# Graph attention on one core: edge values as one product with block-diagonal weights, and sums of two groups in tile pairs

## The chip, the cores and the metric

The kernel runs on one core of a Trainium2 chip. The metric is the device time of one execution in microseconds. Engines are named as the profile names them: PE is TensorE's matrix multiplication and PEld its weight load, DVE is VectorE, ACT is ScalarE, POOL is GpSimd, SP is the engine that issues most DMAs here. SBUF is the working memory of 128 partitions; PSUM is the small memory that PE writes, 128 partitions by 8 banks of 512 f32 values.

## What is computed

There are 6250 nodes with 64 features each and 206250 edges, sorted by destination. The reference, cut to what matters:

```
Qh = (x @ Wq.T + bq).reshape(n, 4, 16)      # Kh, Vh alike
Ee = (edge_attr @ We.T + be).reshape(-1, 4, 16)
score = (Kh[src] * Qh[dst] * (1.0 / np.sqrt(16)) * Ee).sum(-1)
score = jnp.exp(jnp.clip(score, -5.0, 5.0))
msg = Vh[src] * score[..., None]
wV = jax.ops.segment_sum(msg, dst, num_segments=n)
x = layernorm(x + wV.reshape(n, 64))
```

Two pieces matter for the change: the edge values Ee, a product of every edge's 64 attributes with a 64x64 matrix, and the sum of the messages over the edges of one destination.

## The kernel before, in words

Edges are cut into 1612 tiles of 128 edges. Eight tiles make a group, so there are 202 groups, the last with four tiles. Two groups make a step (97 such steps, written s < ONES; after them come 8 steps of one group, which the change leaves alone except for where their operands lie). One long unrolled loop runs over the groups, and the order of all instructions is the order in which the code is written: every engine works through its own queue in that order, and a framework adds the waits on semaphores. It also orders two accesses of different engines to one bank of a PSUM tile, even where they touch different columns.

For group g the work is spread over several turns of the loop (the lines are those of the profile):

- `edges(g)` (line 762) computes the edge values on PE, three turns ahead. The attributes lie transposed: tile 2i in partitions 0 to 63 and tile 2i+1 in partitions 64 to 127 of one 128x128 f32 block `ET`. The result goes to the PSUM region `ee`, of half a bank in each of two banks of the tile `room`. It takes four products: each has a 64x64 block of weights, 64 partitions of attributes and 256 columns (two tiles), and writes 64 partitions; the four use the four quarters of PE's array.
- `biased(g)` (771) adds the bias on ACT and copies to `EB`.
- `queries(g)` (778) computes the query of each edge on PE from a one-hot matrix `TO` (two products into `qq`), `terms(g)` (786) multiplies both on DVE, and `turn(g)` (792) transposes the product back, four 128x128 f32 transposes into `qe`.
- `products`, `weigh`, `message`, `keep` and `take` (820 to 862) form score and message on DVE and ACT. The message is written as three bf16 parts into `MSG`, so 192 columns for a tile.
- `onehot_edges(s)` (798) builds on DVE the one-hot matrices `OH` of a step, 64 destinations wide, by comparing `key` with a row of numbers. `keys` (278) prepares `key` 208 tiles at a time.
- `sums(s)` (874) adds the messages on PE: 16 products, for each of the 8 tile places j one of group 0 and one of group 1, each with 128x64 weights from `OH` and 192 columns of `MSG`. Group 0 writes partitions 0 to 63 and group 1 partitions 64 to 127 of the region `pa`, 192 columns in bank 0 of `room`. The loop gives them out in two halves of eight products.
- `add(s)` (903) reduces `pa` over the three parts on DVE (line 908) into 128x64 and adds it, masked, to two slots of a ring. `fold_blocks` and `add_blocks` (944, 957) carry the ring over to the result through `folded`, in bank 1 of `room`.

All PE products of the loop go through one helper, line 760, so the profile's rows for it are told apart by tile name and shape. The largest of them are the `pick` products: they fetch keys and values of some edges by one-hot matrices, 128x512 bf16, and in the loop they stand between the other products, two units of three products at a time (`picks`, 706). In the order of the queue a turn does: picks, then `turn(g+1)`, picks, `queries(g+2)`, `edges(g+3)`, picks, half of the sums, picks, the other half, picks. About every third turn, eight f32 products of 128 columns (`picked_kv`, 721, rows `pick<-w,x`) come at the turn's start. POOL gathers the other keys and values from memory; SP loads attributes, keys and single rows.

Of the kernel before, what the change touches and what calls it, by code (L numbers as in the profile page):

```python
# [12 lines left out]
AF = mybir.ActivationFunctionType  # L13
OP = mybir.AluOpType
AX = mybir.AxisListType

P = 128
N = 6250
C = 64
# [4 lines left out]
G = 8  # L24
# [3 lines left out]
NS = len(STEPS)  # L28
# [6 lines left out]
NR = P * NB  # L35
RING = 8
STEP = 31
SLACK = 14
SHIFT = STEP
TAIL = STEPS[ONES][0]  # L40
# [17 lines left out]
def tiles_of(g):  # L58
    return min(G, T - g * G)
# [86 lines left out]
def tile_gnn(ctx: ExitStack, tc: tile.TileContext, x, x_blocks, by_rows, xT, wT, bias, beT, weT, eT, src, src_rows,  # L146
             src_single, dst, dst_rows, out):
    nc = tc.nc
# [15 lines left out]
    dst_i = consts.tile([P, T], I32, name="dst_i")  # L164
# [15 lines left out]
    ident = consts.tile([P, P], F32, name="ident")  # L180
# [14 lines left out]
    key_i = consts.tile([P, KEYS], I32, name="key_i")  # L195
# [6 lines left out]
    we_sb = consts.tile([P, 2 * C], F32, name="we_sb")  # L202
# [5 lines left out]
    be_col = consts.tile([P, 1], F32, name="be_col")  # L208
# [13 lines left out]
    ET, QW, at = {}, {}, {}  # L222
    SRC, FROM, ODD, OVER, KB, TO = ({} for _ in range(6))
# [54 lines left out]
    def keys(t0):  # L278

        n = min(KEYS, T - t0)  # L280
        for lo, hi, rows in (t0, min(t0 + n, TAIL * G), C), (max(t0, TAIL * G), t0 + n, P):
            if lo < hi:
                nc.vector.tensor_scalar(key_i[:, lo - t0:hi - t0], dst_i[:, lo:hi], rows - 1, None,
                                        op0=OP.bitwise_and)
        nc.vector.tensor_copy(key[:, t0:t0 + n], key_i[:, :n, None].to_broadcast([P, n, 2]))

    def gather_kv(g, j):
# [29 lines left out]
    with tc.tile_pool(name="nodes", bufs=1) as nodes, \  # L317
# [27 lines left out]
        for i in range(NB // CB):  # L345
            s = slice(i * CB * P, (i + 1) * CB * P)
# [148 lines left out]
        for i in range(NB // CB):  # L495
            bs = slice(i * CB, (i + 1) * CB)
            kv_sb = chunks.tile([P, CB, 2 * C], F32, name="kv_sb")
            for b in range(0, CB, 2):
                two = slice(i * CB + b, i * CB + b + 2)
                ps = npsum.tile([P, 2, 3 * C], F32, name="ps")  # L500
                for u in range(2):
                    c0 = (i * CB + b + u) * P
                    mark.append(nc.tensor.matmul(ps[:, u, :], xT_sb[:, c0:c0 + P], w_sb, start=True,  # L503
                                                 stop=True))
# [137 lines left out]
    with tc.If(rv == 0) as branch:  # L642

        with tc.tile_pool(name="work", bufs=2) as work, \
# [3 lines left out]
            OH, OF, EB, TERM, MSG, SCORE, WEIGHT, HOT = ({} for _ in range(8))  # L648
# [4 lines left out]
            nc.tensor.transpose(still[:, C:C + NB].bitcast(BF16), half_b[:2 * NB].to_broadcast([2 * NB, P]),  # L653
                                ident_b[:2 * NB, :2 * NB])
            room = fixed.tile([P, 2, 4 * P], F32, name="room")
            ee = room[:, :, :2 * P].rearrange("p r (i e) -> p r i e", e=P)
            pa = room[:, 0, 2 * P:2 * P + 3 * C]
            folded = room[:, 1, 2 * P:2 * P + 2 * C].rearrange("p (b c) -> p b c", c=C)
            sum_ = still[:, 2 * P:2 * P + C]
            weights = [still[:, P + k * G * H:P + (k + 1) * G * H]  # L660
                       .rearrange("p (g h) -> p g h", g=G) for k in range(3)]
            px = [fixed.tile([P, 4 * P], F32, name=f"pick{k}") for k in range(2)]
            xs = [accp.tile([P, 4 * P], F32, name=f"x{k}") for k in range(2)]
            qq = fixed.tile([P, G // 2, P], F32, name="qq")
            qe = [fixed.tile([P, G, C], F32, name=f"qe{k}") for k in range(2)]
# [93 lines left out]
            def product(*aps, **kw):  # L759
                mark.append(nc.tensor.matmul(*aps, **kw))  # L760

            def edges(g):

                n = tiles_of(g) // 4
                for u in range(2):
                    for r in range(2):
                        rows = slice(r * C, (r + 1) * C)
                        product(ee[u * C:(u + 1) * C, r, :n, :], we_sb[rows, rows],
                                ET[g][rows, u * n:(u + 1) * n, :], start=True, stop=True)

            def biased(g):

                n = tiles_of(g) // 2
                EB[g] = work.tile([P, G // 2, P], F32, name="eb")
                nc.scalar.activation(EB[g][:, :n].rearrange("p (i r) e -> p r i e", r=2),  # L775
                                     ee[:, :, :n // 2], AF.Identity, bias=be_col)

            def queries(g):

                n = tiles_of(g)  # L780
                for u in range(2):
                    product(qq[u * C:(u + 1) * C, :n // 2, :], QW[g],
                                     TO[g][:, u * n // 2:(u + 1) * n // 2, :],
                                     start=True, stop=True)

            def terms(g):
# [5 lines left out]
            def turn(g):  # L792

                half = tiles_of(g) // 2
                for k in range(half):
                    nc.tensor.transpose(qe[g % 2][:, k:k + half + 1:half, :], TERM[g][:, k, :], ident)  # L796

            def onehot_edges(s):

# [69 lines left out]

            def pa_of(s):  # L870

                return {NS - 3: px[0][:, :3 * C], NS - 2: px[1][:, :C], NS - 1: qq.rearrange("p i e -> p (i e)")[:, :C]}.get(s, pa)

            def sums(s, some=slice(0, G)):
                n = tiles_in(s)
                if s < ONES:
                    for j in range(G)[some]:
                        for u in range(2):
                            t = u * G + j
                            product(pa[u * C:(u + 1) * C], OH[s][:, t, :],  # L880
                                    MSG[s][:, t].rearrange("p i c -> p (i c)"),
                                    start=j == 0, stop=j == G - 1, skip_group_check=True)
                    return
                for j in range(n):
                    product(pa_of(s), (OF if s >= WHOLE else OH)[s][:, j, :],
                            MSG[s][:, j].rearrange("p i c -> p (i c)") if s < WHOLE else MSG[s][:, j, :],
                            start=j == 0, stop=j == n - 1,
                                     skip_group_check=True)
# [14 lines left out]
            def add(s):  # L903
                b = first_row(s) // P
                what = pa_of(s)
                if s < ONES:
                    b = first_row(s) // C
                    nc.vector.tensor_reduce(sum_, what.rearrange("p (i c) -> p c i", i=3), axis=AX.X,  # L908
                                            op=OP.add)
                    for k, mask in ((b, above), (b + 1, below)):  # L910
                        slot = ring[:, k % RING, :]
                        if k in touched:
                            nc.vector.scalar_tensor_tensor(slot, sum_, mask_of(mask, s), slot,
                                                           op0=OP.mult, op1=OP.add)
                        else:
                            nc.vector.tensor_scalar(slot, sum_, mask_of(mask, s), None, op0=OP.mult)
                            touched.add(k)
                    return
                if s < WHOLE:
                    nc.vector.tensor_reduce(sum_, what.rearrange("p (i c) -> p c i", i=3), axis=AX.X,  # L920
                                            op=OP.add)
                    what = sum_
                for k, mask in ((b, above), (b + 1, below)):
                    if 0 <= k < BIG + 1:
                        slot = slot_of(k)
                        nc.vector.scalar_tensor_tensor(slot, what, mask_of(mask, s), slot,
                                                       op0=OP.mult, op1=OP.add)
# [92 lines left out]
            for g in range(NG + 1):  # L1020
# [65 lines left out]
                if g - 1 in ends and now:  # L1086
                    s = ends[g - 1]
# [235 lines left out]
```

## Time and profile before

| what | value |
|---|---|
| median of 3 runs | 2093.89 us |
| lowest and highest | 2090.95 and 2097.44 us |
| the profiled execution, its own time | 2090.01 us |
| its span, first to last instruction | 2088.2 us |
| mean granted TensorE clock | 0.947 |
| matmul records, weight load records | 10216, 10409 |

The profile is of one execution. Its lines of groups read: line, engine, operation, what it writes and reads, for a product rows*columns of the array and partitions x columns of the moving operand, how many; then busy microseconds in all and mean nanoseconds of one; then the engine's idle time just before such instructions and what ended it. A product's duration holds its way through the array, so back to back products overlap: what one costs PE is the distance from its start to the start of the next, which the timeline gives. An f32 product of this kernel leaves two records, two weight loads and two matmuls. "issue" is idle time whose end the profile explains by no semaphore.

### The profile page before, as it was taken

The numbers are of one execution on the slowest core, as the hardware profiler recorded it, in microseconds if no ns is written. First come the engines' busy times: TensorE is split into PE (matmuls) and PEld (weight loads), VectorE is DVE, ScalarE is ACT, GpSimd is POOL, SyncE is SP. The second block draws the span as 40 slices with busy tenths as digits, with TensorE's granted clock in tenths as the row PEclk, the third lists the DMA queues.
The fourth block names the chain that finished last, engine by engine and source line by source line (L and its number), as shares of the span: only waits on it lengthen the run. The fifth ranks groups of instructions, "written<-read, shape, count | busy, mean of one in ns | idle before, by whom it ended". The sixth has DMA issues, their size and how long they took to land.

```text
span 2088.2 us, 34475 instructions
## 1 busy us (share of the span) xinstructions
PE 1759.6 (84%) x10216; PEld 831.4 (40%) x10409; DVE 1538.9 (74%) x2598; ACT 1106.8 (53%) x1882; POOL 1254.1 (60%) x1333
## 2 busy tenths in 40 slices
PE   6588888888888889888898989888988988889994
PEld 6334343343334334333343334434433433334443
DVE  5477777777778678687777767767877787777886
ACT  3455555555555455455555545545655555555564
POOL 6566666666666666656666666656666666666542
PEclk9789999999999999999999999999999999999996
DMA  6524333332333333333233332333323333233320
GB/s 174 190 81 126 87 102 93 94 101 86 96 88 98 102 87 100 95 95 101 86 102 95 88 101 86 100 90 91 101 85 111 95 93 100 80 101 101 104 76 26
DMA packets 118968, 204.21 MB, mean 98 GB/s; under 512 B 57073, under 2 KB 60011, under 8 KB 118657
## 3 DMA queue, kind: packets, MB, share of 16 engines
q1 hardware_dynamic: 75998, 115.38, 17.8%
q0 software_dynamic: 42336, 85.48, 14.7%
q8 instruction: 83, 1.36, 0.3%
q10 hardware_dynamic: 436, 1.04, 0.2%
q14 instruction: 115, 0.94, 0.1%
HBM read 194.19 MB, written 7.59 MB: 97 GB/s over the span
## 4 chain that ended last, share of the span: by engine, by line
PE 70%; issue 13%; DVE 12%; ACT 2%; POOL 1%; another core or an unknown queue 1%; DMA 1%; DVEq 0%; ACTq 0%; POOLq 0%
PE pick L760 50%; PE room L760 11%; PE qe L796 4%; PE qq L760 3%; DVE hot L696 3%; DVE prod L822 1%; DVE msg L862 1%; DVE score L824 1%; POOL kv L289 1%; PE ps L503 1%; DVE term L790 1%; DVE qe L843 1%; DVE qe L862 1%; DVE of L810 1%
## 5 line engine op out<-in xcount | busy, mean ns | idle before, releaser
L289 POOL DMA_INDIRECT kv<-kv_tab,src_i x1283 | 1214.9, 947 | 783.8 <-issue 285.9
L760 PE MATMUL pick<-hot,parts 128*128 128x512 bf16 x4839 | 1241.5, 392 | 93.5 <-issue 84.2
L760 PEld LDWEIGHTS <-parts 128*128 128x128 bf16 x5032 | 469.0, 100 | 676.2 <-issue 252.8
L696 DVE TENSOR_TENSOR hot<-from,still 128x2560 bf16<-128x2560 bf16 (+4 forms) x421 | 488.8, 1165 | 11.2 <-PE qe L796 3.8
L775 ACT ACTIVATE eb<-room,be_col 128x512 f32<-128x512 f32 x202 | 137.3, 680 | 443.1 <-DVE still L908 212.8
L857 ACT ACTIVATE msg<-qe 128x512 bf16<-128x512 f32 x400 | 237.8, 595 | 164.9 <-issue 67.4
L822 DVE TENSOR_TENSOR prod<-kv,qe 128x512 f32<-128x512 f32 x203 | 137.6, 678 | 147.9 <-remote 105.4
L275 ACT ACTIVATE to<-to,one_p 126x1024 bf16<-126x1024 bf16 x198 | 226.3, 1143 | 0.0
L269 ACT ACTIVATE to<-kb,minus_row 126x1024 bf16<-126x1024 uint8 x198 | 224.7, 1135 | 0.0
L908 DVE TENSOR_REDUCE still<-room 128x64 f32<-128x192 f32 x97 | 35.5, 366 | 241.0 <-PE pick L760 102.7
L796 PE MATMUL qe<-ident,term 128*128 128x128 f32 x806 | 129.5, 285 | 82.8 <-DVE term L790 36.2
L829 ACT ACTIVATE score<-score,five_p 128x32 f32<-128x32 f32 x203 | 65.1, 321 | 252.9 <-DVE score L824 154.0
L790 DVE TENSOR_TENSOR term<-eb,qq 128x512 f32<-128x512 f32 x202 | 136.9, 678 | 66.5 <-PE pick L760 33.9
L760 PE MATMUL room<-msg,of 128*64 128x192 bf16 (+1 forms) x1592 | 131.9, 264 | 59.6 <-issue 59.1
L796 PEld LDWEIGHTS qe<-ident,term 128*128 128x128 f32 x806 | 100.2, 146 | 140.2 <-DVE term L790 49.4
L760 PE MATMUL room<-et,we_sb 64*64 64x256 f32 (+1 forms) x1616 | 138.2, 412 | 18.9 <-ACT eb L775 10.9
L824 DVE TENSOR_REDUCE score<-prod 128x32 f32<-128x512 f32 x203 | 138.5, 682 | 7.0
L862 DVE TENSOR_TENSOR msg<-qe,msg 128x512 bf16<-128x512 f32 x200 | 136.6, 683 | 7.0 <-ACT to L275 2.6
L862 DVE TENSOR_TENSOR qe<-qe,msg 128x512 f32<-128x512 f32 x200 | 138.3, 692 | 2.0 <-ACT to L269 1.8
L760 PEld LDWEIGHTS <-of 128*64 128x64 bf16 (+1 forms) x1600 | 74.0, 113 | 163.4 <-issue 162.8
L843 DVE SCALAR_TENSOR_TENSOR qe<-still,kv 128x512 f32<-128x512 f32 x200 | 138.6, 693 | 0.0
L760 PE MATMUL pick<-w,x 128*128 128x128 f32 x544 | 82.4, 285 | 26.3 <-issue 25.7
(158 smaller groups left out, 1062.2 us busy)
## 6 DMA issues: line engine op xcount, KB each, us to landing
et<-in_eT SPq DMA_DIRECT2D x100, 512.0 KB
single<-kv_tab SPq DMA_DIRECT2D x2176, 0.5 KB
kb<-key_tab SPq DMA_DIRECT2D x101, 252.0 KB
kv<-kv_tab,src_i POOLq DMA_INDIRECT x1283
srcs<-in_src_rows SPq DMA_DIRECT2D x68, 256.0 KB
qw<-q_tab SPq DMA_DIRECT2D x202, 15.8 KB
kv_tab<-kv_sb SPq DMA_DIRECT2D x4, 640.0 KB
q_tab<-q SPq DMA_DIRECT2D x5, 480.0 KB
```

Of the source, the lines that this page charges most:

```text
L269: nc.scalar.activation(TO[g][:, :n, :], KB.pop(g)[:, :n * P].rearrange("p (j e) -> p j e", j=n), AF.Square, bias=minus_row3[:3 * W])
L275: nc.scalar.activation(TO[g][:, :n, :], TO[g][:, :n, :], AF.Relu, bias=one_p[:3 * W], scale=-1.0)
L289: return nc.gpsimd.indirect_dma_start(out=kv_of(g)[:, j, :], out_offset=None, in_=kv_tab[:, :], in_offset=bass.IndirectOffsetOnAxis(ap=src ...
L696: nc.vector.tensor_tensor(HOT[k][:, lo_ - lo:hi_ - lo].rearrange("p b (a c) -> p b a c", c=2), pairs(from_)[:, None].to_broadcast(shape), ...
L760: mark.append(nc.tensor.matmul(*aps, **kw))
L790: nc.vector.tensor_mul(TERM[g][:, :n], EB.pop(g)[:, :n], qq[:, :n])
L796: nc.tensor.transpose(qe[g % 2][:, k:k + half + 1:half, :], TERM[g][:, k, :], ident)
L822: nc.vector.tensor_mul(prod, kv_of(g)[:, lo:hi, :C], qe[g % 2][:, lo:hi, :])
L824: nc.vector.tensor_reduce(SCORE[g], prod.rearrange("p g (h d) -> p g h d", h=H), axis=AX.X, op=OP.add)
L843: nc.vector.scalar_tensor_tensor(to.rearrange("p g (h d) -> p g h d", h=H), WEIGHT.pop(g)[:, :, :, None].to_broadcast([P, n, H, D]), LEAST ...
L857: nc.scalar.activation(part, left, AF.Copy)
L862: nc.vector.tensor_sub(left if i == 0 else part_of(g, 2)[1], left, part)
```

## The change

Edge values: `ee` becomes one whole bank of `room`, and one product with the whole 128x128 matrix `we_sb` (We transposed twice on the diagonal, zeros elsewhere; it exists already) takes the 128 partitions of a block and 512 columns, four blocks at once. Tile 2i therefore lands in the lower and tile 2i+1 in the upper 64 partitions of block i. `queries` and `turn` follow that order: the one reads every second tile of `TO`, the other writes two neighbouring tiles of `qe`.

Sums: each product takes a pair of tiles, j of group 0 and j of group 1. The weights are the pair's one-hot matrices side by side (128x128), the moving operand is both tiles' messages (384 columns). Of the 128x384 result the two blocks on the diagonal are wanted, the other two are left unread. `pa` is now 384 columns wide and lies in bank 1 of `room` beside `folded`. `add` reads the two blocks with two reductions of 64 partitions each. `keys` writes the keys in the pairs' order.

```diff
+PA = 3 * C
...
-                nc.vector.tensor_scalar(key_i[:, lo - t0:hi - t0], dst_i[:, lo:hi], rows - 1, None,
-                                        op0=OP.bitwise_and)
+                to, from_ = key_i[:, lo - t0:hi - t0], dst_i[:, lo:hi]
+                if rows == C:
+                    to = to.rearrange("p (s j u) -> p s j u", j=G, u=2)
+                    from_ = from_.rearrange("p (s u j) -> p s j u", j=G, u=2)
+                nc.vector.tensor_scalar(to, from_, rows - 1, None, op0=OP.bitwise_and)
...
-            ee = room[:, :, :2 * P].rearrange("p r (i e) -> p r i e", e=P)
-            pa = room[:, 0, 2 * P:2 * P + 3 * C]
-            folded = room[:, 1, 2 * P:2 * P + 2 * C].rearrange("p (b c) -> p b c", c=C)
+            ee = room[:, 0].rearrange("p (i e) -> p i e", e=P)
+            pa = room[:, 1, :2 * PA]
+            folded = room[:, 1, 2 * PA:2 * PA + 2 * C].rearrange("p (b c) -> p b c", c=C)
...
-                n = tiles_of(g) // 4
-                for u in range(2):
-                    for r in range(2):
-                        rows = slice(r * C, (r + 1) * C)
-                        product(ee[u * C:(u + 1) * C, r, :n, :], we_sb[rows, rows],
-                                ET[g][rows, u * n:(u + 1) * n, :], start=True, stop=True)
+                n = tiles_of(g) // 2
+                product(ee[:, :n, :], we_sb, ET[g][:, :n, :], start=True, stop=True)
...
-                nc.scalar.activation(EB[g][:, :n].rearrange("p (i r) e -> p r i e", r=2),
-                                     ee[:, :, :n // 2], AF.Identity, bias=be_col)
+                nc.scalar.activation(EB[g][:, :n], ee[:, :n], AF.Identity, bias=be_col)
...
-                                     TO[g][:, u * n // 2:(u + 1) * n // 2, :],
+                                     TO[g][:, u:n:2, :],
...
-                    nc.tensor.transpose(qe[g % 2][:, k:k + half + 1:half, :], TERM[g][:, k, :], ident)
+                    nc.tensor.transpose(qe[g % 2][:, 2 * k:2 * k + 2, :], TERM[g][:, k, :], ident)
...
-                        for u in range(2):
-                            t = u * G + j
-                            product(pa[u * C:(u + 1) * C], OH[s][:, t, :],
-                                    MSG[s][:, t].rearrange("p i c -> p (i c)"),
-                                    start=j == 0, stop=j == G - 1, skip_group_check=True)
+                        product(pa.rearrange("p (u i) -> p u i", u=2),
+                                OH[s][:, 2 * j:2 * j + 2, :].rearrange("p u c -> p (u c)"),
+                                MSG[s][:, j::G].rearrange("p u i c -> p u (i c)"),
+                                start=j == 0, stop=j == G - 1, skip_group_check=True)
...
-                    nc.vector.tensor_reduce(sum_, what.rearrange("p (i c) -> p c i", i=3), axis=AX.X,
-                                            op=OP.add)
+                    for u in range(2):
+                        rows = slice(u * C, (u + 1) * C)
+                        nc.vector.tensor_reduce(sum_[rows],
+                                                pa[rows, u * PA:(u + 1) * PA].rearrange("p (i c) -> p c i", c=C),
+                                                axis=AX.X, op=OP.add)
```

More of the change, by code (lines that the diff above doesn't have):

```diff
@@ L870, in pa_of @@
             def pa_of(s):
-                return {NS - 3: px[0][:, :3 * C], NS - 2: px[1][:, :C], NS - 1: qq.rearrange("p i e -> p (i e)")[:, :C]}.get(s, pa)
+                return {NS - 3: px[0][:, :3 * C], NS - 2: px[1][:, :C], NS - 1: qq.rearrange("p i e -> p (i e)")[:, :C]}.get(s, pa[:, :3 * C])
             def sums(s, some=slice(0, G)):
```

## The prediction

> **What bounds the kernel now.** I read the page first: busy time, the clock, the chain that ended last.
>
> ```profile
> span 2088.2 us, 34475 instructions
> PE 1759.6 (84%) x10216; PEld 831.4 (40%) x10409; DVE 1538.9 (74%) x2598; ACT 1106.8 (53%) x1882; POOL 1254.1 (60%) x1333
> ...
> PE   6588888888888889888898989888988988889994
> ...
> PEclk9789999999999999999999999999999999999996
> ...
> PE 70%; issue 13%; DVE 12%; ACT 2%; POOL 1%; another core or an unknown queue 1%; DMA 1%; DVEq 0%; ACTq 0%; POOLq 0%
> ```
>
> PE is the busiest engine and 70% of the chain. Its busy share and its clock are even from the start of the loop to the end (the two rows of slices), so one turn stands for all: the span without its first 100 us, over 202 groups, is about 9.8 us a turn. What is added to PE's queue is therefore paid for in time, unless it fills a wait. So the next view is that of the waits, for PE and for the two rows that the change touches on DVE and ACT:
>
> ```profile
> PE pick L760 <- issue: 109.8, 234, 1.2
> PE room L760 <- issue: 75.3, 107, 2.5
> PE qe L796 <- DVE term L790: 36.2, 22, 10.1
> PE qe L796 <- DVE msg L862: 27.9, 15, 3.7
> PE qe L796 <- issue: 18.2, 12, 9.9
> ...
> PE room L760 <- ACT eb L775: 10.9, 7, 2.8
> ...
> ACT eb L775 <- DVE still L908: 212.8, 60, 7.3
> ```
>
> PE waits 64.1 us for DVE (36.2 + 27.9, 37 times) and stands 203.3 us (109.8 + 75.3 + 18.2) in gaps that no semaphore explains. Third come the groups, shapes kept apart, for the counts:
>
> ```profile
> L760 PE MATMUL pick<-hot,parts 128*128 128x512 bf16 x4839 | 1241.5, 392 | 93.5 <-issue 84.2 <-DVE term L790 1.5
> L760 PE MATMUL room<-et,we_sb 64*64 64x256 f32 x1608 | 137.5, 412 | 18.7 <-ACT eb L775 10.7 <-issue 8.0
> L760 PE MATMUL room<-msg,of 128*64 128x192 bf16 x1552 | 125.9, 263 | 59.6 <-issue 59.1
> L760 PEld LDWEIGHTS pick<-w,x 128*128 128x128 f32 x544 | 73.2, 194 | 48.5 <-issue 38.1 <-ACT over L255 1.5 <-ACT msg L857 1.3
> L760 PEld LDWEIGHTS room<-et,we_sb 64*64 64x64 f32 x1616 | 43.3, 134 | 67.6 <-issue 49.3 <-ACT eb L775 13.4 <-ACT msg L857 1.8
> L908 DVE TENSOR_REDUCE still<-room 128x64 f32<-128x192 f32 x97 | 35.5, 366 | 241.0 <-PE pick L760 102.7 <-PE room L760 51.6 <-PE qe L796 38.8
> ```
>
> Edge products leave 8 records a group (1608 / 201, the short last group apart), sums 16 a step (1552 / 97).
>
> **The products' price on PE** is not in the mean durations, since products overlap. It is in the distances of starts, in the timeline of PE in one turn:
>
> ```profile
> 1004.75 1.24 PE L760 MATMUL pick<-hot,parts 128*128 128x512 bf16 x5 [0.86 <-issue]
> 1005.92 0.52 PE L760 MATMUL room<-msg,of 128*64 128x192 bf16 x8
> 1006.38 0.82 PE L760 MATMUL pick<-hot,parts 128*128 128x512 bf16 x3
> ...
> 1008.14 1.24 PE L760 MATMUL pick<-hot,parts 128*128 128x512 bf16 x5
> 1009.22 0.60 PE L796 MATMUL qe<-ident,term 128*128 128x128 f32 x4
> 1009.66 1.46 PE L760 MATMUL pick<-hot,parts 128*128 128x512 bf16 x6
> 1011.04 0.41 PE L760 MATMUL qq<-to,qw 126*64 126x512 bf16 x2
> 1011.38 0.66 PE L760 MATMUL room<-et,we_sb 64*64 64x256 f32 x8
> 1011.98 0.39 PE L760 MATMUL pick<-hot,parts 128*128 128x512 bf16 x1
> ```
>
> A pick of 512 bf16 columns costs 0.216 us (five from 1008.14 to 1009.22), 0.42 ns a column. Eight edge records cost 0.60 us (1011.38 to 1011.98) although one alone lasts 0.412: the four quarters of the array work at once. The sums do so too: eight products of 192 columns would take 0.65 us one by one (8 x 192 x 0.42 ns), and the next pick starts after 0.46.
>
> For f32 over the whole array, the nearest rows are products of 256 columns near the start, with the clock there beside them (PEclk, 1.00):
>
> ```profile
> 67.67 1.03 PE L583 MATMUL pv<-wkv,xe 128*128 128x256 f32 x4
> 68.54 0.38 PE L574 MATMUL tp<-ident,kv 128*128 128x128 f32 x2
> ...
> 67.67:68.54 0.87, 0.87 (x7) 0.72 (x6) 0.87 (x2) 0.61 (x2) 0.56 (x2) 1.00 0.97 319
> ```
>
> Four records in 0.87 us: 0.2175 us a record of 256 columns. A record of 512 then takes 0.435.
>
> **The change part by part.** *Edge values.* Out: 0.60 us a group. In: one product, two records of 512 columns, 2 x 0.435 = 0.87 us. That is 0.27 us more, times 201 groups, 54 us. The weights are now 128 columns of f32: 194 ns against 134 in the rows of the weight loads. Behind the queries, where the array changes its division, the first load may show: between 0 and 60 ns a group, 0 to 12 us; I take 6.
>
> *Sums.* Out, for a half of eight products: the five picks from 1004.75 end at 1005.83 (5 x 0.216) and the next pick starts at 1006.38, so 0.55 us, 0.09 of it ahead of the first product. In: four products of 384 columns, 4 x 384 x 0.42 ns = 0.65 us with nothing ahead of them, for the picks use the whole array too. 0.10 us more, times 194 halves, 19 us. (With 384 columns a weight load of 128 bf16 columns is covered.) The four pairs alone would need 4 x 192 x 0.42 = 0.32 us of the 0.55, so 0.23 us of each half is the change of division, and the new form saves that; it still loses, as it streams twice the columns.
>
> TensorEngine Tiling (Array Packing) in the Trainium skill, section Key Properties, says that changing the tiling mode drains the engine. That speaks for the change, and the 0.23 us agree. The skill's TensorE: Matmul & The Clock Gate, Part 3, section Measured speedup vs the span model, speaks against it: products on different tiles take about the time of one plus 4 ns for each further one. By that rule alone, without the drain, the edge values would cost 2 x 0.2175 + 0.01 = 0.45 us before, the change 0.42 us a group, an estimate of 85 us in place of 54. I keep the 0.60 of the row.
>
> Both distances were read at clock 1.00, and the span was granted less:
>
> ```profile
> core 0: 2088.2 us, clock 0.947
> ```
>
> (54 + 19) / 0.947 = 77 us, and 83 with the weights.
>
> *Orders and layouts.* `queries`, `turn`, `biased` and `keys` move the same elements in other steps. The four transposes already write two separate runs and cost 0.11 us each (0.44 / 4), half the 0.2175 of a 256-column record as their columns say, so runs cost nothing that shows; `keys` has seven calls. I take 0 for them, bounds of 2 us either way.
>
> *The second reduction.* 97 x 0.366 = 36 us more on DVE. DVE stood idle 241.0 us before that very row, waiting for PE, so it comes early and the sums end last. But the second reduction comes after that wait and delays by 0.37 us what is queued behind it: ring, one-hot matrices for picks, message, the next turn's terms, and through these the transposes. I take 0, because the transposes wait only 37 times in 202 turns; the other end, if no slack is left, is 36 us.
>
> *A wait that goes.* `biased` needs nothing of line 908, yet ACT waited 212.8 us for it: `ee` and `pa` share bank 0. Now they lie in different banks. ACT has room at 53%; what reaches PE is the 10.9 us that edge products waited for `biased`. I take -11, bounds 0 and -11. `pa` now shares a bank with `folded`, whose additions on DVE come once in about four turns and are queued ahead of the sums; nothing for that.
>
> *The waits that the longer queue fills.* The added 0.27 + 0.10 x 194 / 202 = 0.37 us a turn vanish where PE would have waited for DVE anyway: 37 times, -14 us. Bounds 0 and -64.
>
> *The gaps without a cause.* Records of PE fall by 8 - 2 per group for matmuls and as many weight loads, 2424, and by 2 x 8 x 97 = 1552 for the sums: 3976 of 20625, 19%. If gaps came by instruction, 19% of 203 us, 39 us, would go; if by time, none. The rows don't decide: sums carry 59.1 / 1552 = 38 ns a record, picks 84.2 / 4839 = 17, but edge products, the densest, 8.0 / 1608 = 5. I take half, -19; the ends are 0 and, if half of all gaps go, -100.
>
> Sum: 83 + 0 - 11 - 14 - 19 = +39 us on the profiled execution's 2090.01, or 2129. That execution lies 4 us below the median of the runs shown, so 2133.
>
> **The rivals.** *Faster: the gaps were made by dense bursts.* Sixteen sums instructions stand in 0.46 us; if such bursts make the gaps behind them and four long products don't, more goes than I took. For: the 38 ns against 17. Against: the 5 ns of the edge products. It decides from 83 - 11 - 14 = 58 us of vanished gaps, 29% of them. With 100 gone: 2094 + 58 - 100 = 2052. Chance 0.20.
>
> *No change: PE's longer turn is swallowed.* All of the 64.1 us for DVE, 19 of gaps and the 11 for ACT go: 83 - 94 = -11, and with a bit of the reduction's 36 us back it ends near 2094. For: DVE is at 74% and POOL paces some turns. Against: the waits stand in 37 turns, the added work in all. Chance 0.10.
>
> *Slower still: DVE becomes late.* The second reduction's 36 us land in full and no gap goes: 83 - 11 - 14 + 36 = 94, 2188. For: the chain holds 12% DVE. Against: the 241.0 us of idle time before the reduction. Chance 0.08.
>
> That the quarters don't really run at once is excluded: eight f32 records one by one need 8 x 0.2175 = 1.74 us, and the next product starts after 0.60.
>
> **How the numbers follow.** My forecast, slower by about 39 us, has 0.62. About 0.3%, 6 us, is what a measurement of this kernel can tell from no change. Faster: 0.20. Same: 0.10. Slower: 0.62 + 0.08 = 0.70. The upper end: 83 + 6 for the weights' other bound, little relief, 2094 + 89 = 2183, and 2185 with the layouts. The lower end must reach over no change into the faster case, to about 80 gone of the gaps: 2094 + 58 - 80 = 2072; I give 2070. The likeliest case has a range of its own, 2105 to 2185.
>
> **What would show it.** In the profile after: two edge records a group, 128*128 with 512 columns, and 0.87 us from the first to the next pick (0.60 would refute the f32 price); sums of 384 columns 0.16 us apart; two reductions a step, 97 x 2; ACT no longer waiting for them ahead of `biased`; PE's waits for DVE below 64 us; gaps by "issue" near 184 us. PE's busy share should rise above 84%. The forecast is wrong if the gaps fall by over 58 us, or if the transposes' waits for DVE grow.

## The result and the profile after

The changed kernel takes 2073.61 us (median of 4 runs, 2069.58 to 2074.36) against 2092.42 us for the kernel before beside it (4 runs, 2088.44 to 2097.44): ratio 0.991, 95% interval 0.9894 to 0.9925. It is faster by 19 us, where I forecast slower by 39. Every ratio here is of undisturbed executions (two slower ones, 2127 us of the kernel before beside `after_again` and 9184 us of `whole_shared_3`, are left out of them), so it can differ by up to 0.0013 from the ratio of the medians. The profiled execution took 2073.41 us, its span 2071.6, at a mean granted clock of 0.963 instead of 0.947.

From the page after: span, busy time by engine, the granted clock by slices, and the chain that ended last.

```profile
span 2071.6 us, 30705 instructions
PE 1805.4 (87%) x8263; PEld 877.3 (42%) x8421; DVE 1582.5 (76%) x2695; ACT 1106.6 (53%) x1882; POOL 1251.9 (60%) x1333
...
PEclk9799999999999999999999999999999999999995
...
PE 43%; DVE 13%; issue 4%; ACT 1%; DMA 1%; another core or an unknown queue 1%; SPq 0%; DVEq 0%; POOL 0%; ACTq 0%; POOLq 0%
```

PE works longer (1805.4 us against 1759.6) and yet the span is shorter: the time came out of PE's idle stretches. The chain says less on this than it seems to: after the change its shares add up to 63%, so it was followed back over the last part of the span only. "Issue" has 4 of these 63, or 7% of the part that was followed, against 13% before. The view of the waits of the same kernel, each row with total, times and longest:

```profile
PE qe L795 <- DVE term L789: 96.5, 52, 9.4
PE qe L795 <- issue: 36.2, 33, 3.0
PE pick L764 <- issue: 31.4, 62, 1.3
PE qe L795 <- DVE msg L861: 16.9, 8, 4.4
...
PE room L764 <- ACT eb L775: 13.6, 13, 5.0
PE room L764 <- issue: 13.5, 21, 1.4
...
ACT eb L775 <- DVE still L908: 255.9, 65, 8.3
```

Gaps without a cause: 31.4 + 13.5 + 36.2 = 81.1 us, where 203.3 stood before: 122 us gone. PE's waits for DVE: 96.5 + 16.9 = 113.4 us, up by 49 from 64.1. ACT's wait for line 908 didn't go (212.8 before, 255.9 now).

The groups after, shapes kept apart, show the products as forecast: two edge records a group, sums of 384 columns, two reductions a step.

```profile
L764 PE MATMUL pick<-hot,parts 128*128 128x512 bf16 x4874 | 1201.7, 385 | 32.7 <-issue 24.8
L764 PE MATMUL room<-et,we_sb 128*128 128x512 f32 x402 | 237.9, 675 | 20.5 <-ACT eb L775 13.4 <-issue 6.9
L764 PE MATMUL room<-msg,of 128*128 128x384 bf16 x776 | 159.1, 326 | 6.4 <-issue 6.1
L908 DVE TENSOR_REDUCE still<-room 64x64 f32<-64x192 f32 x194 | 71.0, 366 | 196.5 <-PE pick L764 74.1 <-PE room L764 59.5 <-PE qe L795 51.7
```

What the products cost PE, by distances of starts in its timeline:

```profile
1000.24 1.13 PE L764 MATMUL room<-et,we_sb 128*128 128x512 f32 x2
1001.20 4.05 PE L764 MATMUL pick<-hot,parts 128*128 128x512 bf16 x18
...
1017.45 1.24 PE L764 MATMUL pick<-hot,parts 128*128 128x512 bf16 x5
1018.53 0.81 PE L764 MATMUL room<-msg,of 128*128 128x384 bf16 x4
1019.18 2.10 PE L764 MATMUL pick<-hot,parts 128*128 128x512 bf16 x9
```

Edge values: 0.96 us (1000.24 to 1001.20). Half of the sums: 0.65 us (1018.53 to 1019.18), with nothing ahead of them, for the five picks before them take 1.08 = 5 x 0.216. Medians of such distances over all groups: edge values 0.595 before and 0.963 after, a half of the sums with its entry 0.763 and 0.866. So (0.368 x 202) + (0.103 x 194) = 74 + 20 = 94 us of PE work were added; 77, or 83 with the weights, were forecast. The account of the span, in us: work +94, gaps -122, waits for DVE +49, PE's wait for `biased` +3. That leaves +24, where the span shows -17.

The 41 us between them lie in the main inside PE's busy time, in the picks, whose own fell by 40 us (1241.5 before, in the prediction's rows, to 1201.7). As a rule a pick starts 0.216 us after the one before it. Of the distances from one pick to the next, 184 (of 4173) were about 0.43 us before, in stretches where the granted clock was one half, and 82 (of 4208) after: 22 us less. Another 125 were longer than 0.46 us before and 35 after. A pick's record lasts about 0.38 us, so of each of these 0.16 us counts as busy and stands in no row of waits, 17 us less in all. The clock stood at one half for 224 us of the span before and 157 after.

So the price was paid, and something about the gaps paid it back. What are these gaps? In the kernel before, the timeline of all engines shows what goes on behind the half of the sums that starts at 1005.92 (its row stands in the prediction: 0.52 us):

```profile
1008.14 0.81 PE L760 MATMUL pick<-hot,parts 128*128 128x512 bf16 x3
1008.20 0.37 DVE L908 TENSOR_REDUCE still<-room 128x64 f32<-128x192 f32 x1 [1.53 <-PE pick L760]
1008.27 0.94 POOL L289 DMA_INDIRECT kv<-kv_tab,src_i  x1 [1.00 <-PE pick L760]
1008.60 0.69 ACT L775 ACTIVATE eb<-room,be_col 128x512 f32<-128x512 f32 x1 [2.45 <-DVE still L908]
```

The sums ended by 1006.44 (1005.92 + 0.52), yet the reduction that waits for PE starts only at 1008.20, 1.8 us later. POOL, which also waits for PE, comes free 0.07 us after DVE, as if signals had been held up and then let go together; ACT follows when the reduction is done. Counting, behind the span's first 100 us, stretches of over 2 us in which at least two of PE's signalling instructions ended and none of their signals is recorded, the trace before has 272 (1076 us in all) and the trace after 298 (1155 us). The change therefore did not remove this condition; it made it cost less.

### The profile page after: what moved, and what is told of

Its sections match the earlier page's. It is cut to its first block, busy times and chain, and to the rows that moved or that the text cites. A ratio compares the mean times of both kernels' runs of the same rounds, so it can differ in the third digit from the quotient of the medians.

```text
span 2071.6 us, 30705 instructions
## 1 busy us (share of the span) xinstructions
PE 1805.4 (87%) x8263; PEld 877.3 (42%) x8421; DVE 1582.5 (76%) x2695; ACT 1106.6 (53%) x1882; POOL 1251.9 (60%) x1333
## 3 DMA queue, kind: packets, MB, share of 16 engines
q0 software_dynamic: 42336, 85.48, 14.7%
q10 hardware_dynamic: 436, 1.04, 0.2%
## 4 chain that ended last, share of the span: by engine, by line
PE 43%; DVE 13%; issue 4%; ACT 1%; DMA 1%; another core or an unknown queue 1%; SPq 0%; DVEq 0%; POOL 0%; ACTq 0%; POOLq 0%
PE pick L764 29%; PE room L764 10%; PE qe L795 3%; DVE hot L700 3%; PE qq L764 2%; DVE prod L821 1%; DVE term L789 1%; DVE score L823 1%; DVE still L908 1%; DVE msg L861 1%; DVE qe L842 1%; DVE qe L861 1%; DVE of L809 1%; DMA kv<-kv_tab,src_i 1%
## 5 line engine op out<-in xcount | busy, mean ns | idle before, releaser
L764 PE MATMUL pick<-hot,parts 128*128 128x512 bf16 x4874 | 1201.7, 385 | 32.7 <-issue 24.8
L764 PEld LDWEIGHTS <-parts 128*128 128x128 bf16 x5032 | 495.5, 99 | 627.2 <-issue 175.8
L775 ACT ACTIVATE eb<-room,be_col 128x512 f32<-128x512 f32 x202 | 137.3, 680 | 460.5 <-DVE still L908 255.9
L795 PE MATMUL qe<-ident,term 128*128 128x128 f32 x806 | 135.3, 291 | 150.2 <-DVE term L789 96.5
L764 PE MATMUL room<-et,we_sb 128*128 128x512 f32 x404 | 239.1, 675 | 20.7 <-ACT eb L775 13.6
L908 DVE TENSOR_REDUCE still<-room 64x64 f32<-64x192 f32 x194 | 71.0, 366 | 196.5 <-PE pick L764 74.1
L764 PE MATMUL room<-msg,of 128*128 128x384 bf16 (+1 forms) x816 | 165.1, 326 | 6.4 <-issue 6.1
L861 DVE TENSOR_TENSOR qe<-qe,msg 128x512 f32<-128x512 f32 x200 | 137.8, 689 | 13.6 <-ACT msg L856 7.2
L764 PEld LDWEIGHTS <-of 128*128 128x128 bf16 x824 | 81.4, 100 | 81.8 <-issue 12.4
L764 PEld LDWEIGHTS room<-et,we_sb 128*128 128x128 f32 x404 | 63.6, 198 | 72.5 <-issue 47.9
```

Of the source, the lines that this page charges most:

```text
L795: nc.tensor.transpose(qe[g % 2][:, 2 * k:2 * k + 2, :], TERM[g][:, k, :], ident)
L861: nc.vector.tensor_sub(left if i == 0 else part_of(g, 2)[1], left, part)
```

## The experiments

**Theories.** "Many": the gaps come by the number of PE's instructions in such bursts, and the change helps because it has fewer. "Divided" (or quarters): they come from products on parts of the array. "Banks": the gain comes from the two regions of `room` that no longer share a bank. Against all three stood the plain price: PE's added work is paid for. These experiments ran on five chips. On two of them the kernel before took 1718 us, on the other three 2065 to 2093, and every ratio is to the kernel before beside it on the same chip.

**Each part alone: `edges_only`** has the new edge values and the sums of before:

```diff
-product(pa..., OH[s][:, 2 * j:2 * j + 2, :]..., MSG[s][:, j::G]...)
+for u in range(2):
+    t = u * G + j
+    product(pa[u * C:(u + 1) * C, :PA], OH[s][:, t, :], MSG[s][:, t]...)
 ... (the order of the keys and the one reduction are those of before as well)
```

> The edge values' part of the change alone: one product of 128 rows, sums as before (sixteen products of 64 weights and 192 columns, one reduction). On PE's queue this costs 0.963 - 0.595 = 0.37 us a group, 74 us. Theory 'many': PE's gaps without a cause (203 us before, 81 after) come with the number of PE instructions; 2424 of the 3976 that the change removes go here, so about 0.61 x 122 = 74 us of gaps go, and the time is near 2090. Rival 'divided': the gaps come with products on parts of the array; the sums, which hold most of the gaps for their number, stay divided, so gaps stay over 150 us and the time is 2110 to 2150.

Measured: 2076.57 us, ratio 0.9947 (0.9932 to 0.9962): 11 us faster (0.0053 x 2090.26). Gaps 50.7 + 47.6 + 26.9 = 125 us. The edge values, the dearer part (74 us of PE work), bring most of the gain.

**`sums_split`** is the changed kernel with each pair's product cut into its two groups: the whole array, but twice the instructions.

```diff
-product(pa..., MSG[s][:, j::G]..., start=j == 0, ...)
+for u in range(2):
+    product(pa[:, u * PA:(u + 1) * PA], OH[s][:, 2 * j:2 * j + 2, :]...,
+            MSG[s][:, u * G + j]..., start=j == 0 and u == 0, ...)
```

> The change with each sums product cut in two of 192 columns: the whole array and the same columns and PE time as after, but as many sums instructions as before (1552 records more). Theory 'many': gaps rise from 81 to about 130 us, time 2085 to 2110. Rival 'divided': nothing is divided, gaps stay at 81 and the time at 2074, within 6 us.

Measured: 2082.06 us, 0.9966 (0.995 to 0.9983), gaps 105 us. Of the whole change's 0.009 more than half (0.0056) is lost by cutting the sums into twice as many records, with the same array and the same columns.

**`edges_split`** cuts the edge product into four, one for each block of 128 columns; **`both_split`** cuts both.

```diff
-product(ee[:, :n, :], we_sb, ET[g][:, :n, :], start=True, stop=True)
+for i in range(n):
+    product(ee[:, i:i + 1, :], we_sb, ET[g][:, i:i + 1, :], start=True, stop=True)
```

> The change with the edge product cut in four of 128 columns: whole array, same columns, but as many edge instructions as before (2424 records more). Theory 'many': gaps rise from 81 to about 155 us, time 2095 to 2125. Rival 'divided': gaps and time as after, 81 us and 2074, within 6 us.

> Both cuts at once: as many PE instructions as before, no product on a part of the array in sums and edge values, PE time of the columns as after. Theory 'many': gaps near 200 us as before, and time 2110 to 2180, since the price on PE's queue (94 us by the distances of starts) is paid with nothing won. Rival 'divided': gaps 81 us, time 2074 within 8 us.

Measured: `edges_split` 2081.88 us, 0.9961 (0.9947 to 0.9975), gaps 129 us; `both_split` 2095.64 us, 1.0029 (1.0017 to 1.0041), gaps 139 us. With both products cut there are as many instructions as before (34831 against 34668), no product uses a part of the array where the change had removed it, and the gain is gone. The gaps came back only in part: 139 us, not the 203 of before. In all four runs so far the measured time lies outside what both theories gave and below "many": that theory still took PE's added work as paid. From the waits of `both_split`:

```profile
PE pick L764 <- issue: 66.0, 115, 1.9
PE room L764 <- issue: 46.1, 74, 1.5
PE qe L796 <- DVE term L790: 40.1, 25, 5.6
PE qe L796 <- issue: 27.1, 17, 11.4
```

Its timeline of PE shows what a gap looks like from inside:

```profile
1003.24 0.82 PE L764 MATMUL room<-msg,of 128*128 128x192 bf16 x8
1004.05 0.38 PE L764 MATMUL pick<-hot,parts 128*128 128x512 bf16 x1
1004.78 0.38 PE L764 MATMUL pick<-hot,parts 128*128 128x512 bf16 x1 [0.35 <-issue]
1005.49 0.39 PE L764 MATMUL pick<-hot,parts 128*128 128x512 bf16 x1 [0.33 <-issue]
1006.91 0.81 PE L764 MATMUL pick<-hot,parts 128*128 128x512 bf16 x3 [1.04 <-issue]
```

Single picks 0.7 us apart (1004.05, 1004.78, 1005.49) where picks follow each other after 0.216 otherwise: in this stretch an instruction's own length hardly counts. The gaps by "issue" look here like a PE that is fed slowly.

**What feeds PE slowly? `before_nogather` and `after_nogather`** leave out POOL's gathers of keys and values from the fifth step on; the rest works on what the buffers hold.

```diff
-elif now and step_of[g] + KVB - 1 < NS:
+elif False and now and step_of[g] + KVB - 1 < NS:
```

> The kernel before, with the gathers of keys and values left out from the fifth step on (about 1280 of them become some 80; the old contents of the buffers are used, so the result is another). Theory 'paced': the gathers and what they hold up set the pace, and PE's gaps and waits only fill what PE has left over. Then the time falls by over 100 us, gaps to under 60 us. Rival 'dense': PE's own bursts of short instructions make the gaps, gathers or not; the time falls by under 40 us and the gaps stay over 150.

> The changed kernel with the same gathers left out. Theory 'paced': PE now sets the time alone, and the change costs its price on PE's queue (0.37 us x 202 + 0.10 us x 194 = 94 us): slower than the kernel before without gathers by 60 to 110 us. Rival 'dense': the order stays as with gathers, this one 10 to 30 us faster than the other.

Measured: 1740.24 us and 1831.19 us beside the kernel before at 2093.21 (ratios 0.8319, 0.83 to 0.8339, and 0.8756, 0.8734 to 0.8778). Without the gathers the order turns round: the changed form is 91 us slower, close to the price of 94. The page and the waits of `before_nogather`:

```profile
PE 1639.7 (94%) x10216; PEld 808.8 (46%) x10409; DVE 1524.2 (88%) x2598; ACT 1104.1 (63%) x1882; POOL 75.0 (4%) x86
```

```profile
PE qe L796 <- issue: 11.3, 2, 11.0
PE pick L760 <- issue: 10.4, 65, 0.2
...
PE room L760 <- issue: 2.5, 4, 1.2
```

and the waits of `after_nogather`:

```profile
PE qe L795 <- DVE term L789: 35.7, 29, 5.6
...
PE room L764 <- ACT eb L775: 5.9, 3, 5.3
```

With POOL at 75 us of work, the gaps are 24 us in place of 203, and PE is busy 94% of the span; there what it is given costs time. PE's own bursts of short instructions are the same as before, so they alone don't make the gaps. The held-up stretches number 0 before and 2 (10 us) after, against 272 and 298 with gathers. With its gathers the kernel before is 353 us longer; the changed one some 243 (its 0.991 of that chip's 2093.21, less 1831.19). The hold-up hangs on the gathers, and the changed kernel loses less to it.

**Is it the array's division? `quarters_whole_sums`** keeps the four quarter products of the edge values, and lets sixteen sums products use the whole array, in two banks with two reductions.

```diff
-product(pa[u * C:(u + 1) * C], OH[s][:, t, :], MSG[s][:, t]...)
+product(pas[u], OH[s][:, 2 * j:2 * j + 2, :]..., MSG[s][:, u * G + j]...)
 ... (keys and reductions as in the change; `folded` moves to another tile)
```

> The kernel before with its edge products on quarters, and sums as sixteen products of a pair's 128 weights and 192 columns, so as many instructions as before and no half arrays in the sums. Price on PE: (0.876 - 0.763) x 194 = 22 us. Theory 'many' (gaps by number): nothing is won, 2092 + 22 = about 2114. Theory 'paced': PE has slack, 2085 to 2098. Rival 'divided': the sums' gaps go (59 us), 2050 to 2070.

Measured: 2102.09 us, 1.0045 (1.0028 to 1.0061), gaps 98.8 + 45.4 + 44.3 = 189 us. The time lies between "paced" and "many" and far from "divided". Undividing the sums without having fewer of them brings nothing.

**`one_reduce`** is the changed kernel without its second reduction: one reduction of 128 partitions over the first group's columns, so the second group's sums are left out.

```diff
-for u in range(2): ... tensor_reduce(sum_[rows], pa[rows, u * PA:(u + 1) * PA]...)
+nc.vector.tensor_reduce(sum_, pa[:, :PA].rearrange("p (i c) -> p c i", c=C), ...)
```

> The changed kernel with one reduction of 128 partitions over the first 192 columns of the sums, so the second group's sums are left out: what the second reduction costs (36 us on DVE). If DVE's chain through the transposes sets the pace after the change (96.5 us of waits for it), 2045 to 2062. If the reduction is hidden behind the wait for the sums, 2068 to 2076.

Measured: 2067.61 us, 0.9885 (0.9863 to 0.9907), against 0.991 with it: the difference is 0.0025, about 5 us of the reduction's 36, with intervals that overlap.

**Banks, and PE work for nothing.** `whole_shared` is the kernel before with whole-array edge products, in the two halves of banks where they lay, beside `pa`: two products a group instead of four. `edges_halves` is the changed kernel with the edge product cut into two column halves of the array. `spacer` is the kernel before with one more f32 product a group ahead of the edge values, overwritten by them.

```diff
 # whole_shared
-for u in range(2):
-    for r in range(2): product(ee[u * C:(u + 1) * C, r, :n, :], we_sb[rows, rows], ...)
+for r in range(2):
+    product(ee[:, r, :n, :], we_sb, ET[g][:, r * n:(r + 1) * n, :], start=True, stop=True)
 # edges_halves
-product(ee[:, :n, :], we_sb, ET[g][:, :n, :], start=True, stop=True)
+for u in range(2):
+    cols = slice(u * C, (u + 1) * C)
+    product(ee[cols, :n, :], we_sb[:, cols], ET[g][:, :n, :], start=True, stop=True)
 # spacer
+product(room[:, 0, :2 * P]..., we_sb, ET[g][:, :2, :], start=True, stop=True)
 ... (in whole_shared `biased`, `queries` and `turn` follow the new order)
```

> The kernel before with its places in PSUM, its sums and its keys, but the edge values as two products of the whole array and 256 columns, one in each of the two banks, beside the sums and the fold. Price on PE as for one whole product, about 75 us. Theory 'quarters' (the four small products bring on what the gathers then cost): as edges_only, 2070 to 2085. Rival 'banks' (what was won is that edge values and sums lie in different banks): nothing is won, 2092 plus most of the 75, 2130 to 2170.

> The changed kernel with the edge product cut in two halves of the array's columns (128 rows, 64 weights, 512 columns each, at the same time): the PE time of the whole product, but a divided array. Theory 'divided': the loss by the gathers rises from 242 us towards 350, 2100 to 2180. Rival 'time' (what helps is that PE is busy 0.37 us longer at that place, however): 2070 to 2082.

> The kernel before with one product more ahead of each group's quarter products: the whole array, 256 f32 columns, overwritten by what follows; about 0.45 to 0.5 us of PE a group, 90 to 100 us. Theory 'time': PE's time at that place is free, since the gathers' loss shrinks by as much: 2080 to 2105. Theory 'quarters': the quarters keep their loss of 350 us and the added time is paid: 2160 to 2195.

Measured, with the kernel before at 1718.22 us there: 1780.96 (1.0372, 1.0355 to 1.039), 1803.91 (1.0504, 1.0486 to 1.0521) and 1828.09 (1.0642, 1.0624 to 1.0659). All three pay most of their work: 63, 86 and 110 us, where the distances of starts give 75, 74 and 127. That couldn't decide between the theories, for on this chip the kernel before was as fast as without gathers; no trace of it there is kept, but those of these three have gaps of under 2 us. The changed kernel once more, on a chip with the slower kernel before:

> The changed kernel once more, beside the kernel before on the same chip. The chip of the call before this one ran the kernel before in 1718 us and showed none of the held-up semaphores. Theory 'held up': the sign hangs on whether the gathers hold up the semaphores on that chip. Where the kernel before takes about 1718 us, the change pays its whole price on PE, 1800 to 1825; where it takes about 2092, the change is 10 to 25 us faster, as first measured. Rival 'chip apart': the change is faster on either by about 0.9%.

Measured: 2045.95 us against 2065.62, 0.9903 (0.9886 to 0.9921). The gain holds. It is the chip of the runs without gathers, where the kernel before took 2093 us at another time. Then, on another chip:

> The changed kernel beside these three. Theory 'held up': 0.99 of the kernel before where that takes 2065 us or more; 1.048 to 1.06 where it takes about 1718.

> As whole_shared, wanted on a chip where the kernel before takes 2065 to 2095 us. Theory 'quarters': as the edge part of the change alone, 0.99 to 1.0 of the kernel before. Rival 'banks': slower than before by 40 to 75 us. Where the kernel before takes 1718 us: 1781 again.

> As edges_halves, wanted on the same kind of chip. Theory 'divided': slower than the whole product by over 25 us, 1.005 to 1.04 of the kernel before. Rival 'time': as the change, 0.985 to 0.995. Where the kernel before takes 1718 us: 1804 again.

> As spacer, wanted on the same kind of chip. It adds 0.63 us of PE a group, 127 us by the distances of starts (1.224 against 0.595). Theory 'time' (PE's time is free there while something else holds the loop up): under 1.015 of the kernel before. Theory 'quarters': the added time is paid, 1.04 to 1.065. Where the kernel before takes 1718 us: 1828 again.

Here the kernel before took 1718.29 us again, and: the changed kernel 1820.15 (1.0594, 1.0576 to 1.0612), `whole_shared` 1779.77 (1.0362, 1.0345 to 1.038), `edges_halves` 1803.61 (1.0498, 1.0481 to 1.0516), `spacer` 1829.5 (1.0647, 1.0629 to 1.0665). The same changed kernel that won by 19 us loses by 102. Its page and its waits there:

```profile
PE 1734.5 (96%) x8263; PEld 872.5 (48%) x8421; DVE 1573.8 (87%) x2695; ACT 1104.7 (61%) x1882; POOL 1254.9 (69%) x1333
```

```profile
PE qe L795 <- DVE term L789: 42.6, 32, 5.6
...
PE pick L764 <- issue: 1.4, 9, 0.2
PE qe L795 <- issue: 1.3, 1, 1.3
```

POOL does all its gathers (1254.9 us), and yet the gaps are 2.7 us: the gathers alone don't make the hold-up, something else must be added to them. Neither this trace nor that of `spacer` here holds one held-up stretch. The transfers themselves are not slower with the hold-up: in the changed kernel the 42336 packets of the gathers last 115 ns each in the mean with it and 115 without, the 68 packets that bring in instructions 1072 and 1053.

Last, two of them on a chip with the hold-up:

> As whole_shared_2, still wanted on the same kind of chip. Theory 'quarters': 0.985 to 1.0 of the kernel before. Rival 'banks': 1.02 to 1.04. Where the kernel before takes 1718 us: 1.036 again.

> As spacer_2, still wanted where the kernel before takes 2065 us or more. Theory 'time': under 1.015 of the kernel before. Theory 'quarters': 1.04 to 1.065. Where the kernel before takes 1718 us: 1.065 again.

Measured beside 2091.11 us: `whole_shared` 2081.96 (0.9964, 0.9949 to 0.9979), `spacer` 2100.89 (1.0049, 1.003 to 1.0068). The first wins 8 us with `ee` and `pa` still sharing a bank, against 11 in `edges_only` with overlapping intervals, so "banks" falls as what the gain needs. The second adds 0.629 us a group by the same medians of start distances, x 202 = 127 us of PE work, and pays 10 us for it, as "time" said, far below the 1.04 of "quarters"; the same product cost 111 us where nothing was held up. From the waits of `spacer` with the hold-up:

```profile
PE pick L760 <- issue: 105.9, 257, 2.4
PE room L760 <- issue: 45.9, 80, 1.8
PE qe L798 <- DVE term L792: 28.8, 23, 5.3
PE qe L798 <- issue: 17.6, 9, 10.4
...
PE qe L798 <- DVE msg L864: 8.5, 5, 3.1
```

The gaps are 169 us in place of some 203, and PE's waits for DVE 37 in place of 64: waits took up some 61 of the 127. The rest is in no wait. Some of it shows in the picks again: where a pick starts more than 0.23 us after the one before it, the picks' busy time beyond 0.216 us each adds up to 46 us here, and to 79 in the kernel before.

**All kernels with the hold-up together.** Differences to the kernel before, each with its ratio times 2092.42 us; instructions as recorded, with the pick records that a trace lacks added (34668 before):

| kernel | instructions | PE work added, us | time, us |
|---|---|---|---|
| the change | -3805 | +94 | -19 |
| one_reduce | -3976 | +94 | -24 |
| edges_only | -2424 | +74 | -11 |
| sums_split | -2253 | +96 | -7 |
| whole_shared_3 | -1616 | +75 | -8 |
| edges_split | -1389 | +101 | -8 |
| both_split | +163 | +103 | +6 |
| quarters_whole_sums | +194 | +22 | +9 |
| spacer_3 | +808 | +127 | +10 |

(The added work is by medians of distances, as above: an edge product costs 0.963 us whole, 0.995 in four, 0.968 in two and 1.224 with the spacer, against 0.595; half of the sums 0.866 in the change and 0.876 in sixteen products, against 0.763.) Over these nine and the kernel before, the time goes with the number of instructions at a correlation of 0.97, 6.6 ns for each; with the added PE work the correlation is -0.19. This relation was found after the runs, each time is known to about 3 us, and a product brings its weight load and often a smaller width with it, so the number of instructions is what the time went with, not yet a cause taken alone. The gaps follow it less well: `whole_shared` with 137 us of them is faster than before, `both_split` with 139 slower.

## Why the prediction was wrong

The step that failed is "What is added to PE's queue is therefore paid for in time, unless it fills a wait." It was drawn from a PE that is 84% busy and evenly so. On chips with the hold-up, time hardly follows PE's work: 127 us added cost 10, and known waits took up only some 61 of them. It is paid where nothing is held up (+102 us for the change) and without gathers (+91), and there my 77 to 83 was the right sum in kind. The trace that I read was of the other condition, and the evenness said nothing on it. That 2073.61 lies above 2070, the lower end that I gave, owes to the rival for which that end was put there; the likeliest case ran from 2105 to 2185.

- *The edge values* were forecast at +0.27 us, 0.30 with the weights, and cost +0.368 (0.595 to 0.963). The 0.87 was the streaming alone; 0.09 us more shows, above my bound of 60 ns for the weights. Whether it is the load of 128 f32 columns was not separated.
- *The sums*: +0.10 us forecast, +0.103 measured. Right.
- *The array's division*: the timeline of PE in `edges_halves`, whose edge products use column halves as the queries before them do, prices one change of it:

```profile
1001.62 0.41 PE L764 MATMUL qq<-to,qw 126*64 126x512 bf16 x2
1001.86 1.03 PE L764 MATMUL room<-et,we_sb 128*64 128x512 f32 x4
1002.82 1.47 PE L764 MATMUL pick<-hot,parts 128*128 128x512 bf16 x6
```

The queries take 0.24 us where the edge product stays in their division (1001.62 to 1001.86); in the changed kernel, where it doesn't, the median is 0.337: 97 ns a change. In the kernel before, whose quarters follow the same queries, the median is 0.337 too. That agrees with what TensorEngine Tiling (Array Packing) in the Trainium skill, section Key Properties, says, that changing the tiling mode drains the engine.

- *The wait that goes*, -11 us: wrong. ACT's wait for line 908 grew to 255.9 us with the banks apart, and PE's for `biased` from 10.9 to 13.6. The shared bank was not what made that row; with the banks apart ACT still follows line 908 (65 times), so something else orders the two, and in the stretch shown line 908 itself starts late. What orders them was not tried.
- *The waits that the longer queue fills*, -14 us: wrong in sign. PE's waits for DVE grew by 49 us. My own mark, "or if the transposes' waits for DVE grow", spoke for slower; here they grew in a faster kernel, perhaps because DVE is held up too and PE now arrives earlier. The same kernel's longest row of them is 42.6 us without the hold-up and 96.5 with it, which fits; no run took it alone.
- *The second reduction*: 0 taken, about 5 us measured, within the noise and far from the other end of 36.
- *The gaps*: 19 us taken by half of the share of records, 122 went. This is the term whose size turned the sign, together with the picks inside PE's busy time, which the sum had no term for. I had a rival for it, "the gaps were made by dense bursts", with 58 us as its point of decision, at 0.20; its time of 2052 was too good mainly because DVE's waits took back 49 of what went, where 14 less of them had been taken. Its mechanism is borne out in part: fewer and longer products do lose less, and `both_split` loses the gain again when they are cut. But the bursts alone make no gaps (`before_nogather`), and whether it is their density or the mere number of instructions was not separated: the kernels with more instructions are also those with denser bursts.

What the runs show: the hold-up needs the gathers and appears on some chips; time in it goes with the number of instructions; banks and PE's work don't explain the gain. That undividing the array is not what brings it is borne out by `both_split`, `quarters_whole_sums` and `sums_split`; `edges_halves` could have shown it most directly, but it ran only where nothing was held up. Nearly all of the changed instructions are PE's, so instructions of other engines were not priced. What stays open is what the hold-up is. In it the trace also lacks signals: 7187 updates by DMAs are recorded for the changed kernel with it, 32952 for the same kernel without. Recording may therefore be part of the cause and not only of the picture: every time here comes with a recorded span and clock, so none shows a kernel without recording. Nor did any run show why chips differ, or whether it is the chip at all: only one was met at two times, with the hold-up at both.

## What to carry to other kernels

A busy share of 84% says that an engine is used, not that its work sets the time: when "issue" gaps of 200 us stand beside it, add a useless product first and see whether it is paid for. Where many signals come free together and single instructions start at a distance well above their own cost, try fewer instructions even at the price of more columns; in this kernel that paid. And a gain got in such a condition is to be measured on more than one chip: this change is worth -19 us on one and +102 us on another.

## What had not been expected of the hardware

The same program took 2092 us on one chip and 1718 on another, with the same gathers. With the hold-up, picks came 0.7 us apart in the stretch shown, instead of 0.216, and a reduction started 1.8 us after the products that it waited for. It is tied to POOL's gathers: without them, 353 us of 2093 were gone. The granted clock was lower with it, 0.947 to 0.970 against 0.979 to 0.988, but not by the size of the gaps: 0.963 stands beside 81 us of them, 0.967 beside 169 and 0.970 beside 139.
